# Experts of a mixture run in order of their load, with fewer rows for the less loaded ones

## The chip, the cores and the metric

The kernel runs on one core of one Trainium2 chip. The metric is the device time of one execution in microseconds, lower is better. A core has five engines that run side by side, each with a queue of its own that it works through in order: TensorE (PE in the profile) multiplies matrices, VectorE (DVE) and ScalarE (ACT) work element by element, GpSimd (POOL) does the same more slowly and issues gathers and scatters, SyncE (SP) issues transfers. Sixteen DMA engines move the data that those queues ask for. An instruction that must wait holds up everything behind it on its engine.

## The reference

The input has four batches of 512 tokens with 512 features. Three parts follow one another: a cross-attention of the normalised input, an attention block of 16 causal heads, and a mixture of experts. Only the last part is touched here. With T = 2048 tokens, 16 experts (E), 6 choices for each token (K) and a hidden width of 352 (I) it is:

```python
logits = t @ gate_w.T
probs = jax.nn.softmax(logits, axis=-1)
topv, topi = jax.lax.top_k(probs, K)
topv = topv / jnp.sum(topv, axis=-1, keepdims=True)
...
hh = jax.nn.silu(g) * u          # g = t @ eg_w[e].T, u = t @ eu_w[e].T
routed = jnp.einsum('eti,edi,te->td', hh, ed_w, cw)
shared = jax.nn.silu(t @ sg_w.T) * (t @ su_w.T) @ sd_w.T
out = x + (routed + shared).reshape(b, s, d)
```

Each token goes to its six best experts and, besides, through one shared expert of hidden width 704. On average an expert gets 2048 x 6 / 16 = 768 tokens.

## The kernel before

Every matmul is done in float16 with the operands split into a high and a low part, three products for one (`mm3`, L76 to L85: high x high, high x low, low x high). So each weight and each intermediate result is split by ScalarE, which writes the high part, and VectorE, which writes the low one (`split`, L69 to L71; `split1`, L73 to L75).

**Routing.** For each batch `route1` normalises the tokens, writes them split into `h2p` and transposes them into `h2T`. `route2` computes the logits on TensorE, the softmax (its Exp on ScalarE is L508) and the six best experts of each token. `route3` counts: a matmul with a triangular matrix gives each token its place among the tokens of an expert. `slot` is the row of the token in `xs_d`, a DRAM buffer with 2048 rows for each expert, `tid` the expert, `cw` the factor; each has one column for each of the six choices, in rising order of the expert's number. `macc` is the running count of tokens for each expert. GpSimd then scatters the rows to `xs_d` with one indirect DMA for 128 tokens and one choice (`scatter`, L452).

**Capacity.** An expert's rows are worked through up to a fixed number, `CAP` = 832. What is over goes through a conditional block at the end (`extra`, 60 blocks of 128 rows under a branch on `tot`), whose row and weight numbers are worked out on the chip from the counts (L848 to L892). It isn't entered unless an expert has more than 832 tokens.

**The expert loop** (L1073 and following). Experts run in the order of their number. For each, `static_weights` loads three pieces of weights with SP (L844) into `est` and splits them into `wt`, `wb` and `dt` on ScalarE and VectorE; `rows_in` has SP transpose the expert's rows from `xs_d` into `xT`, in two halves of 384 and 448 rows. `gate_up_rows` does, for each half, the gate and up projections (68 matmuls, with the rows as columns: 384 or 448 wide) and the product silu(g) x u; `down_rows` the down projection, nine 512-wide matmuls for each 128 rows and six for the 64 rows left over (L981), after which VectorE adds two parts (L984, L985). SP stores each block to `y_d`. The weights and rows of the next expert are fetched while one is worked on.

**Gathers.** Since a token's choices stand in rising order of the expert, its k-th choice is known to be stored once expert 10 + k is through. So from expert 11 on GpSimd gathers, for each of 16 groups of 128 tokens, one choice for each expert that is worked on (L1043), and VectorE adds it, times its factor, to the result (L1052). The sixth choice comes after the last expert.

**The shared expert** fills gaps: `shared(1, half)` and `shared(2, half)` lie between the routing of the last batch and expert 0, batch 3's at the end. In each half ScalarE does six Silus (L688), VectorE six products (L692 to L695) and both six splits (L73 to L75). Gate results take three PSUM banks in turn (tag `a`), up results two (tag `w`), so TensorE can run ahead of VectorE by that much only.

**What sets the order.** A scheduler places the instructions on each engine's queue by its own estimate of times; `after(x, y)` makes x stand behind y, and `pin` keeps an instruction in the order of the program. Buffers of a tag are taken in turn, and whoever writes one waits for the last reader of it.

Of the kernel before, what the change touches and what calls it, by code (L numbers as in the profile page):

```python
# [17 lines left out]
P = 128  # L18
# [13 lines left out]
SR = SI - 5 * P  # L32
LB = T // P
CAP = 832
FB = CAP // P
HB = CAP - FB * P
CUTS = (0, FB // 2 * P, CAP)
CW = CAP - CUTS[1]
ON = 60
ROWS = E * T + 1  # L40

# [11 lines left out]
def xattn_moe_block_kernel(ctx: ExitStack, tc: tile.TileContext, x, xT, ctxT, wqkx, bqk, ln1, ln2,  # L53
# [17 lines left out]
                nc.vector.scalar_tensor_tensor(lo, src, scale, hi, ALU.mult, ALU.subtract))  # L71

    def split1(hi, lo, src, eng=nc.vector):  # L73
        nc.scalar.activation(hi, src, AF.Copy)
        eng.tensor_tensor(lo, src, hi, ALU.subtract)  # L75

    def mm3(o, terms, start=True, stop=True, hold=None):
        n = len(terms)
# [54 lines left out]
    wo_d = [dram.tile([P, 2 * HG * D], F16, name=f"wo_d{g}") for g in range(G)]  # L133
    xs_d = dram.tile([ROWS, 2 * D], F16, name="xs_d")
    r_d = [dram.tile([P, NT, D], F32, name=f"r_d{b}") for b in range(B)]
    y_d = dram.tile([E * CAP + 1, D], F32, name="y_d")
    yo_d = dram.tile([ROWS, D], F32, name="yo_d")

    cw = const.tile([P, B * NT, K], F32, name="cw")
# [350 lines left out]
    def route2(b):  # L490
# [14 lines left out]
        nc.vector.tensor_reduce(mx, lgv, AX.X, ALU.max)  # L505
        pr = rp.tile([P, NT, E], F32, name="gpr", bufs=1)
        nc.vector.tensor_tensor(pr, lgv, mx.unsqueeze(2).to_broadcast([P, NT, E]), ALU.subtract)
        nc.scalar.activation(pr, pr, AF.Exp, scale=PSC)  # L508
        sm = rp.tile([P, NT], F32, name="gsm", bufs=1)
        nc.vector.tensor_reduce(sm, pr, AX.X, ALU.add)  # L510
        rc = rp.tile([P, NT], F32, name="grc", bufs=1)
# [160 lines left out]
    def gate_up(b, half, hid, tmp):  # L672
        shw = shx["w"]
        cl = slice(half * SH, (half + 1) * SH)
        hs = hid().rearrange("p (i a s) -> p i a s", i=6, a=2)
        for ic in range(6):
            R = P if ic < 5 else SR

            def proj(ps, a):
                o0 = ic * 8 * P + a * C * P  # L680
                mm3(ps, [(shw[:, 0, o0 + c * P:o0 + (c + 1) * P], shw[:, 1, o0 + c * P:o0 + (c + 1) * P],
                          h2T[b][:, c, cl], h2T[b][:, C + c, cl]) for c in range(C)])

            t = tmp()
            sg, hf = t[:, :SH], t[:, SH:]
            pg = bank("a", f"sg{b}_{half}_{ic}")[:, :SH]
            proj(pg, 0)
            nc.scalar.activation(sg[:R], pg[:R], AF.Silu, scale=PSC)  # L688
            if ic < 5:
                pu = bank("w", f"su{b}_{half}_{ic}")[:, :SH]  # L690
                proj(pu, 1)
                nc.vector.scalar_tensor_tensor(hf[:R], pu, GS * PSC, sg[:R], ALU.mult, ALU.mult)  # L692
            else:
                nc.vector.tensor_scalar(hf[:R], pg[R:2 * R], GS * PSC, None, ALU.mult)
                nc.vector.tensor_tensor(hf[:R], hf[:R], sg[:R], ALU.mult)  # L695
            split1(hs[:R, ic, 0], hs[:R, ic, 1], hf[:R])
            if ic == 5:
                nc.scalar.activation(hs[R:2 * R, ic, 0], hf[:R], AF.Copy)
        return hs
# [102 lines left out]
    route2(B - 1)  # L802
    route3(B - 1)
    scatter(B * NT * K)
    for half in range(2):
        shared(1, half)

    rctx.close()
    xin = ctx.enter_context(tc.tile_pool(name="xin", bufs=3, reuse_waits="tile"))
# [4 lines left out]
    GA = G2 - HB  # L814
    NA = C * GA

    def part(dsts, src, n, first=False):
        st_ = mw.tile([P, IP * 4], F32, tag="est", name="est", bufs=3)
        src(st_[:, :n])
        o = 0  # L820
        for hi, lo in dsts:
            w = math.prod(hi.shape[1:])
            v = st_[:, o:o + w]
            if len(hi.shape) == 3:
                v = v.rearrange("p (a b) -> p a b", a=hi.shape[1])
            for ins in split(hi, lo, v, WS):
                if first:
                    pin(ins)
            o += w

    def weights(load, first=False):
        wt = mw.tile([P, 2, NA], F16, name="wt")
        wb = mw.tile([P, C, 2, HB], F16, name="wb")
        dt = mw.tile([P, 2, 3 * D], F16, name="dt")
        for j in range(2):
            cl, ca = slice(j * 2, j * 2 + 2), slice(j * 2 * GA, (j + 1) * 2 * GA)
            part([(wt[:, 0, ca], wt[:, 1, ca]), (wb[:, cl, 0], wb[:, cl, 1])],
                 lambda o, j=j: load(o, (ew0, ew1)[j]), 2 * G2, first)
        part([(dt[:, 0], dt[:, 1])], lambda o: load(o, ed), 3 * D, first)
        return wt, wb, dt  # L840

    def static_weights(e):
        def load(dst, src):
            nc.sync.dma_start(dst, src[e * P:(e + 1) * P, :])  # L844
        return weights(load, e == 0)

    cps = bank("s", "cnt")
    nc.tensor.matmul(cps[:, :E], onesm, macc, start=True, stop=True)  # L848
    cnt = ms1.tile([P, E], F32, name="cnt")
    nc.vector.tensor_copy(cnt, cps[:, :E])  # L850
    NL = LB - FB
    thr = ms1.tile([P, NL], F32, name="thr")
    nc.vector.tensor_scalar(thr, ioe[:, FB:], float(P), float(CAP), ALU.mult, ALU.max)
    gt = ms1.tile([P, E, NL], F32, name="gt")
    nc.vector.tensor_tensor(gt, cnt.unsqueeze(2).to_broadcast([P, E, NL]),
                            thr.unsqueeze(1).to_broadcast([P, E, NL]), ALU.is_gt)
    mt = ms1.tile([P, E], F32, name="mt")
    nc.vector.tensor_reduce(mt, gt, AX.X, ALU.add)
    cs = mt
# [34 lines left out]
    xts = {}  # L894

    def rows_in(e, h):
        lo, hi = CUTS[h], CUTS[h + 1]
        t = xts[e, h] = xin.tile([P, 2 * C, hi - lo], F16, tag="xT", name="xT")
        flip(t, xs_d[1 + e * T + lo:1 + e * T + hi, :])

    nxt = static_weights(0)
    rows_in(0, 0)
    rows_in(0, 1)
    for half in range(2):
        shared(2, half)

    sf, tf = (v.rearrange("p t k -> p (t k)") for v in (slot, tid))
    rk, lt = (ms1.tile([P, B * NT * K], F32, name=nm) for nm in ("rkk", "rlt"))
    yru = ms1.tile([P, B * NT, K], U32, name="yru")
    yrc = ms1.tile([P, B * NT, K], U32, name="yrc")  # L910
    nc.vector.scalar_tensor_tensor(rk, tf, -float(T), sf, ALU.mult, ALU.add)
    nc.vector.tensor_scalar(lt, rk, float(CAP + 1), None, ALU.is_lt)
    nc.vector.scalar_tensor_tensor(rk, tf, float(CAP), rk, ALU.mult, ALU.add)
    nc.vector.tensor_tensor(rk, rk, lt, ALU.mult)
    nc.vector.tensor_copy(yrc.rearrange("p t k -> p (t k)"), rk)
    nc.vector.tensor_tensor(lt, sf, lt, ALU.mult)
    nc.vector.tensor_tensor(lt, sf, lt, ALU.subtract)
    nc.vector.tensor_copy(yru.rearrange("p t k -> p (t k)"), lt)

    RI = (P, P, I - 2 * P)  # L920
    pend = []
# [49 lines left out]
    def down_rows(dt, hT, lo, n, ll, put):  # L971
        ps = bank("s", f"y{lo}")
        yt = mp.tile([P, D], F32, name="yt")
        if n == P:
            mm3(ps, [(hT[:R, ic, lo:lo + P], hT[:R, ic, ll:ll + P],
                      dt[:R, 0, ic * D:(ic + 1) * D], dt[:R, 1, ic * D:(ic + 1) * D]) for ic, R in enumerate(RI)])
            nc.scalar.activation(yt, ps, AF.Copy, scale=1.0 / (GS * WS))
        else:
            for ic, R in enumerate(RI):
                for a in range(2):  # L980
                    nc.tensor.matmul(ps, hT[:R, ic, lo:lo + 2 * n], dt[:R, a, ic * D:(ic + 1) * D],  # L981
                                     start=ic == a == 0, stop=ic == 2 and a == 1)
            y2 = mp.tile([P, D], F32, tag="sb", name="y2")
            nc.scalar.activation(y2[:n], ps[n:], AF.Copy, scale=1.0 / (GS * WS))  # L984
            nc.vector.scalar_tensor_tensor(yt[:n], ps[:n], 1.0 / (GS * WS), y2[:n], ALU.mult, ALU.add)  # L985
        put(yt[:n])

# [5 lines left out]
    def expert(wd, e):  # L993
# [3 lines left out]
            return lambda yt: nc.sync.dma_start(y_d[r:r + yt.shape[0], :], yt)  # L997

        for h in range(2):
            w = CUTS[h + 1] - CUTS[h]  # L1000
            half = w % P
            hT = gate_up_rows(wt, wb, xts.pop((e, h)), w, half, tick)
            flush(tick)
            for lo in range(0, w, P):
                pend.append((dt, hT, lo, min(P, w - lo), w + half + lo, put(1 + e * CAP + CUTS[h] + lo)))
            yield

    def extra(o):
# [29 lines left out]
        ring.update(n=0, w=w, new=new, keep=keep)  # L1038

    def gather():  # L1040
        k, idx, src, tt = todo.pop(0)
        yg = place()
        nc.gpsimd.indirect_dma_start(out=yg, out_offset=None, in_=src,  # L1043
                                     in_offset=bass.IndirectOffsetOnAxis(ap=idx[:, tt, k:k + 1], axis=0))
        gathered.append((k, tt, yg))
        add(ring["keep"])

    def add(keep):
        while len(gathered) > keep:
            k, tt, yg = gathered.pop(0)  # L1050
            acc = residual(tt // NT)[:, tt % NT]
            pin(nc.vector.scalar_tensor_tensor(acc, yg, cw[:, tt, k:k + 1], acc, ALU.mult, ALU.add))  # L1052
            if k == K - 1 and tt not in late:
                store(tt, acc)

# [3 lines left out]
        if keep is not None:  # L1059
            add(keep)  # L1060

    def want(k, idx, src, tts=range(B * NT)):
        todo.extend((k, idx, src, tt) for tt in tts)

    def tick():
        left = ring["steps"]
# [6 lines left out]
    for e in range(E):  # L1073
        wd = nxt
        for h, _ in enumerate(expert(wd, e)):
            if h == 0 and e > E - K:
                gather_all()
                want(e - (E - K) - 1, yrc, y_d[:1 + e * CAP, :])
                ring["steps"] = 13
            if e + 1 < E:  # L1080
                rows_in(e + 1, h)
                if h == 0:
                    nxt = static_weights(e + 1)
    gather_all(0)
    lookahead(lambda: xin.tile([P, 3, D], F32, tag="xT", name="yg"), 3, 7)
    hs = shared_up(B - 1, 0)
    flush()
    want(K - 1, yrc, y_d)
    gather_all()
    shared_down(B - 1, 0, hs)  # L1090
    hs = shared_up(B - 1, 1)
# [4 lines left out]
    if stop is None or stop == "all":  # L1096
        rv = nc.values_load(tot[0:1, 0:1], min_val=0, max_val=E * NL)
        with tc.If(rv > 0):
            for o in range(ON):
                extra(o)  # L1100
            for k in range(K):
                want(k, yru, yo_d)
            gather_all(0)


# [61 lines left out]
```

## Time and profile before

| | us |
|---|---|
| median of the timed runs | 1899.01 (1898.14 to 1901.34) |
| profiled execution | 1826.83 |
| its span, first to last instruction | 1825.1 |
| mean granted TensorE clock in it | 0.985 |
| TensorE busy | 1747.9 |
| VectorE busy | 1122.9 |
| ScalarE busy | 843.8 |
| GpSimd busy | 441.0 |

All views of the trace are of the one profiled execution. Places in it are in us from the span's start. A line such as L844 is a line of the kernel's file; where a helper like `split` or `mm3` issues an instruction, the line is the helper's, so the three products of `mm3` stand under L80, L83 and L84. A row of groups names engine, operation, output and inputs, shape, count, busy time and mean duration; a row of waits names who waited for whom, the sum, how often and the longest. TensorE's instructions overlap: their durations are longer than the distance from one start to the next. "Clock" is the share of full speed that TensorE was granted.

### The profile page before, as it was taken

Reading aid. Unit: us, or ns where it says so; the run is one execution under the profiler, and the core shown is the slowest. Engines: PE = TensorE matmul, PEld = TensorE weight load, DVE = VectorE, ACT = ScalarE, POOL = GpSimd, SP = SyncE. Lnnn points to the kernel's source line nnn. Section 1 sums busy time; section 2 is a strip of 40 time slices with the busy share of each in tenths; the row PEclk is TensorE's granted clock in tenths of the full one; section 3 lists DMA queues with packets and bytes.
Section 4 is the critical chain, followed back from the end, with each engine's and each line's share of the span. In section 5 each row is a group of like instructions: output and inputs, shape, how many; then the busy total and the mean of one; then the engine's idle time right before and its main releaser. Section 6 shows DMA issues by size and latency. Waiting matters only on the chain. (4 is left out here: it accounts for less than half of the span.)

```text
span 1825.1 us, 28676 instructions
## 1 busy us (share of the span) xinstructions
PE 1747.9 (96%) x10483; PEld 990.7 (54%) x10483; DVE 1122.9 (62%) x2784; ACT 843.8 (46%) x1769; POOL 441.0 (24%) x522
## 2 busy tenths in 40 slices
PE   8899899999999999899999999899999999999997
PEld 3555455555555555556556757555555555554554
DVE  6887777777776667666667545344334434456655
ACT  4655645465534545445455522345444444444322
POOL 5423011130345353000003635000000000044553
PEclk9999999999999999999999999999999999999999
DMA  7978668574678578534446646455555565599756
GB/s 237 242 157 226 148 145 188 149 193 95 142 170 237 146 160 237 102 66 94 100 97 143 182 120 208 130 145 149 166 156 150 140 176 142 147 246 234 204 171 209
DMA packets 398294, 298.78 MB, mean 164 GB/s; under 512 B 339840, under 2 KB 340096, under 8 KB 397376
## 3 DMA queue, kind: packets, MB, share of 16 engines
q1 hardware_dynamic: 365024, 182.81, 43.0%
q0 software_dynamic: 33120, 114.06, 19.8%
q8 instruction: 84, 1.38, 0.3%
q14 instruction: 66, 0.54, 0.1%
HBM read 124.81 MB, written 90.18 MB: 118 GB/s over the span
## 5 line engine op out<-in xcount | busy, mean ns | idle before, releaser
L1043 POOL DMA_INDIRECT yg<-y_d,yrc x96 | 107.6, 1121 | 577.9 <-DVE hf L946 470.4
L627 ACT ACTIVATE pe<-pe,bnm 128x128 f32<-128x128 f32 (+3 forms) x256 | 142.4, 557 | 160.7 <-DVE bnm L625 160.0
L80 PE MATMUL qk<-hT,wqk 128*128 128x512 f16 (+1 forms) x520 | 196.2, 377 | 3.8 <-DMA hT<-hh 3.8
L84 PE MATMUL qk<-hT,wqk 128*128 128x512 f16 (+1 forms) x520 | 196.3, 377 | 0.0
L83 PE MATMUL qk<-hT,wqk 128*128 128x512 f16 (+1 forms) x520 | 196.2, 377 | 0.0
L71 DVE SCALAR_TENSOR_TENSOR pn<-pe,brc,pn 128x128 f16<-128x128 f32 (+3 forms) x256 | 147.4, 585 | 21.8 <-ACT pn L70 18.8
L625 DVE CUSTOM_DVE_ANT_0 pe<-sc,causal 128x128 f32<-128x128 f32 (+3 forms) x256 | 117.1, 485 | 58.5 <-PE sc L622 58.0
L70 ACT ACTIVATE pn<-pe,brc 128x128 f16<-128x128 f32 (+3 forms) x256 | 133.5, 553 | 30.6 <-ACT pe L627 18.5
L80 PE MATMUL v<-wv,hT 128*128 128x256 f16 x512 | 139.7, 273 | 0.9 <-DMA hT<-hh 0.9
L83 PE MATMUL v<-wv,hT 128*128 128x256 f16 x512 | 139.7, 273 | 0.0
L84 PE MATMUL v<-wv,hT 128*128 128x256 f16 x512 | 139.6, 273 | 0.0
L80 PE MATMUL g<-xT,wt 128*128 128x384 f16 (+1 forms) x384 | 130.3, 339 | 0.0
L83 PE MATMUL g<-xT,wt 128*128 128x384 f16 (+1 forms) x384 | 130.3, 339 | 0.0
L84 PE MATMUL g<-xT,wt 128*128 128x384 f16 (+1 forms) x384 | 130.2, 339 | 0.0
L932 ACT ACTIVATE hT_e<-hf 128x384 f16<-128x384 f32 (+2 forms) x96 | 52.6, 548 | 141.1 <-DVE hf L946 140.2
L70 ACT ACTIVATE qkt<-qk 128x512 f16<-128x512 f32 x128 | 74.8, 586 | 80.2 <-PE qk L84 79.3
L80 PE MATMUL y<-dt,hT_e 128*128 128x512 f16 (+1 forms) x288 | 109.9, 382 | 0.0
L84 PE MATMUL y<-dt,hT_e 128*128 128x512 f16 (+1 forms) x288 | 109.2, 379 | 0.0
L83 PE MATMUL y<-dt,hT_e 128*128 128x512 f16 (+1 forms) x288 | 109.1, 379 | 0.0
L659 DVE SCALAR_TENSOR_TENSOR x<-wo,x 128x512 f32<-128x512 f32 x128 | 87.4, 686 | 29.5 <-PE wo L84 28.9
L80 PE MATMUL av<-pt,vt 128*128 128x512 f16 (+3 forms) x256 | 78.5, 307 | 26.8 <-DMA pt<-pn 13.9
L452 POOL DMA_INDIRECT xs_d<-h2p,slotu x96 | 96.6, 1006 | 28.8 <-issue 26.7
(293 smaller groups left out, 4204.1 us busy)
## 6 DMA issues: line engine op xcount, KB each, us to landing
y_d<-yt SPq DMA_DIRECT2D x96, 256.0 KB, 2.8
est<-in_ew_dram SPq DMA_DIRECT2D x32, 704.0 KB, 6.5
est<-in_ed_dram SPq DMA_DIRECT2D x16, 768.0 KB, 4.2
wqk<-wqk_d POOLq DMA_DIRECT2D x20, 512.0 KB, 4.5
wqk_st<-in_wqk_dram SPq DMA_DIRECT2D x16, 512.0 KB, 4.2
wqk_d<-wqk POOLq DMA_DIRECT2D x15, 512.0 KB, 5.5
xs_d<-causal POOLq DMA_DIRECT2D x16, 384.0 KB, 6.4
wv<-wv_d POOLq DMA_DIRECT2D x10, 512.0 KB, 4.1
```

The lines of the kernel that those rows point to most:

```text
L70: return (nc.scalar.activation(hi, src, AF.Copy, scale=scale), nc.vector.scalar_tensor_tensor(lo, src, scale, hi, ALU.mult, ALU.subtract))
L71: nc.vector.scalar_tensor_tensor(lo, src, scale, hi, ALU.mult, ALU.subtract))
L80: ins = nc.tensor.matmul(o, lh, rh, start=start and j == 0, stop=False)
L83: nc.tensor.matmul(o, lh, rl, start=False, stop=False)
L84: ins = nc.tensor.matmul(o, ll, rh, start=False, stop=stop and j == n - 1)
L452: ins = nc.gpsimd.indirect_dma_start(out=xs_d, out_offset=bass.IndirectOffsetOnAxis(ap=slotu[:, tt, k:k + 1], axis=0), in_=h2ps[tt], in_of ...
L625: nc.vector.tensor_tensor_reduce(pe, ps[:, :w], causal[:, S - w:], -1.0, 3e38, ALU.add, ALU.min, nm)
L627: nc.scalar.activation(pe, pe, AF.Exp, bias=nm, scale=-1.0, accum_out=sm)
L659: nc.vector.scalar_tensor_tensor(x2[:, t, :], ps, 1.0 / (VS * WS), x2[:, t, :], ALU.mult, ALU.add)
L932: nc.scalar.activation(hT[:R, ic, :w], hf, AF.Copy)
L1043: nc.gpsimd.indirect_dma_start(out=yg, out_offset=None, in_=src, in_offset=bass.IndirectOffsetOnAxis(ap=idx[:, tt, k:k + 1], axis=0))
```

## The change

The experts are ranked on the chip by their count of tokens, the fullest first. The loop runs over ranks, and the rank decides how many rows are worked through: 832 for ranks 0 to 2, 800 for 3 to 9, 768 for 10 to 15. Which expert has a rank is read into registers of SP (`seat`), and the addresses of the weight loads and of the row transposes are worked out from them. Since results lie in `y_d` in order of rank, each token's six rows and factors are sorted by rank before the gathers. The Exp of the last batch's routing softmax and the splits of the second expert's weights get another place in the order. The diff, cut to its core ("...": left out):

```diff
-FB = CAP // P
-HB = CAP - FB * P
-CUTS = (0, FB // 2 * P, CAP)
-CW = CAP - CUTS[1]
+STEPS, DC = (3, 10), 32
+CAPS = [CAP - DC * sum(r >= s for s in STEPS) for r in range(E)]
+OFFS = [1 + sum(CAPS[:r]) for r in range(E + 1)]
+FB = min(CAPS) // P
+CUT = FB // 2 * P
+CW = CAP - CUT
+HB = 64
...
     scatter(B * NT * K)
+
+    cps = bank("s", "cnt")
+    nc.tensor.matmul(cps[:, :E], onesm, macc, start=True, stop=True)
+    cnt = const.tile([P, E], F32, name="cnt")
+    nc.vector.tensor_copy(cnt, cps[:, :E])
+    key = rp.tile([P, E], F32, tag="gmx", name="key", bufs=1)
+    nc.vector.scalar_tensor_tensor(key, cnt, float(E), ioe, ALU.mult, ALU.subtract)
+    sq = rp.tile([P, E, E], F32, tag="w4", name="sq", bufs=1)
+    nc.vector.tensor_tensor(sq, key.unsqueeze(1).to_broadcast([P, E, E]),
+                            key.unsqueeze(2).to_broadcast([P, E, E]), ALU.is_gt)
+    rank = const.tile([P, E], F32, name="rank")
+    nc.vector.tensor_reduce(rank, sq, AX.X, ALU.add)
...
+    nc.vector.tensor_reduce(whof, sq, AX.X, ALU.add)
+    who = const.tile([1, E], I32, name="who")
+    nc.vector.tensor_copy(who, whof[0:1, :])
...
     for half in range(2):
         shared(1, half)
+    after(zz["exp"], zz["silu", 1, 0, 1])
...
-            for ins in split(hi, lo, v, WS):
-                if first:
+            for j, ins in enumerate(split(hi, lo, v, WS)):
+                if order == 0:
                     pin(ins)
+                elif order == 1:
+                    after(ins, zz["hs", 2, 1][j])
...
-    def static_weights(e):
+    here = {}
+
+    def seat(r):
+        here[r] = nc.values_load(who[0:1, r:r + 1], engines=[mybir.EngineType.SP], min_val=0, max_val=E - 1)
+
+    def ranked_weights(r):
         def load(dst, src):
-            nc.sync.dma_start(dst, src[e * P:(e + 1) * P, :])
-        return weights(load, e == 0)
+            nc.sync.dma_start(dst, src[bass.ds(here[r] * P, P), :])
+        return weights(load, r)
...
     def rows_in(e, h):
-        lo, hi = CUTS[h], CUTS[h + 1]
-        t = xts[e, h] = xin.tile([P, 2 * C, hi - lo], F16, tag="xT", name="xT")
-        flip(t, xs_d[1 + e * T + lo:1 + e * T + hi, :])
+        lo, n = h * CUT, CAPS[e] - CUT if h else CUT
+        t = xts[e, h] = xin.tile([P, 2 * C, n], F16, tag="xT", name="xT")
+        flip(t, xs_d[bass.ds(here[e] * T + (1 + lo), n), :])
...
+    n = NT * K
+    for b in range(B):
+        oh = mp.tile([P, CW], F32, tag="sg", name="roh")[:, :n * E].rearrange("p (n e) -> p n e", e=E)
+        ts = slice(b * n, (b + 1) * n)
+        nc.vector.tensor_tensor(oh, tf[:, ts].unsqueeze(2).to_broadcast([P, n, E]),
+                                ioe.unsqueeze(1).to_broadcast([P, n, E]), ALU.is_equal)
+        nc.vector.tensor_tensor(oh, oh, rank.unsqueeze(1).to_broadcast([P, n, E]), ALU.mult)
+        nc.vector.tensor_reduce(rt[:, ts], oh, AX.X, ALU.add)
+    nc.vector.scalar_tensor_tensor(yr, rt, float(CAP), rk, ALU.mult, ALU.add)
+    for s_ in STEPS:
+        nc.vector.tensor_scalar(lt, rt, -float(s_), 0.0, ALU.add, ALU.max)
+        nc.vector.scalar_tensor_tensor(yr, lt, -float(DC), yr, ALU.mult, ALU.add)
...
+    for t in range(B * NT):
+        nc.vector.max(m8[:, t, :], ng[:, t, :])
+    nc.vector.tensor_scalar(m8, m8, -1.0, None, ALU.mult)
+    nc.vector.tensor_copy(yrc, m8[:, :, :K])
...
+        nc.vector.tensor_tensor(eq, yv[:, ts].unsqueeze(2).to_broadcast([P, NT, K, K]),
+                                m8[:, ts, :K].unsqueeze(3).to_broadcast([P, NT, K, K]), ALU.is_equal)
+        nc.vector.tensor_tensor(eq, eq, cw[:, ts].unsqueeze(2).to_broadcast([P, NT, K, K]), ALU.mult)
+        nc.vector.tensor_reduce(cws[:, ts], eq, AX.X, ALU.add)
...
-            w = CUTS[h + 1] - CUTS[h]
+            w = CAPS[e] - CUT if h else CUT
...
-                want(e - (E - K) - 1, yrc, y_d[:1 + e * CAP, :])
+                want(e - (E - K) - 1, yrc, cws, y_d[:OFFS[e], :])
...
             if e + 1 < E:
+                if h == 0:
+                    seat(e + 1)
                 rows_in(e + 1, h)
                 if h == 0:
-                    nxt = static_weights(e + 1)
+                    nxt = ranked_weights(e + 1)
```

In the order that the scheduler makes of it, the sixteen register loads of SP stand together: the first ahead of rank 0's weight loads, the other fifteen right behind these, ahead of the first row transposes. The two first `roh` products stand in VectorE's queue among the last steps of `route1`, ahead of the last batch's last transpose; the rest of the ranking and sorting stands between the reduction of `tid` (L569 before) and the splits of rank 0's weights, among the products and splits of shared(1) and shared(2). The matmuls of the loop, the scatters and the gathers keep their order.

## The prediction

> **What bounds the kernel now.** I read the page first, then the chain that ended last, then TensorE's waits by stage, then stretches of the span, then single instructions. The page says TensorE:
>
> ```profile
> PE 1747.9 (96%) x10483; PEld 990.7 (54%) x10483; DVE 1122.9 (62%) x2784; ACT 843.8 (46%) x1769; POOL 441.0 (24%) x522
> ```
>
> An average over stages decides nothing, so the expert stage next. In the chain of work, in order of time, the six matmuls of an expert's last 64 rows (L981) come back at an even beat; the stretch between two of them is one expert. The columns of the second view are busy time and count of PE, PEld, DVE, ACT, POOL, then granted clock, DMA share, GB/s.
>
> ```profile
> 1331.89 1.30 PE y L981 x6
> 1368.78 1.30 PE y L981 x6
> ```
>
> ```profile
> 1331.89:1368.78 36.89, 36.89 (x197) 19.14 (x196) 15.36 (x25) 16.78 (x29) 0.00 (x0) 1.00 0.56 153
> 1627.03:1663.93 36.90, 36.90 (x198) 19.15 (x196) 22.57 (x36) 15.79 (x28) 17.79 (x15) 1.00 0.98 248
> ```
>
> One expert is 36.89 us, TensorE never pauses, the clock is full, every other engine is busy at most 61%. Here a column less is time less. In the second row, with gathers running, the DMA engines are 0.98 busy: little is spare. What a column costs is the distance of starts in the timeline (us, duration, line, operation):
>
> ```profile
> 1339.83 0.35 PE L83 MATMUL u<-xT,wt 128*128 128x448 f16 x1
> 1340.02 0.35 PE L84 MATMUL u<-xT,wt 128*128 128x448 f16 x1
> ...
> 1351.13 0.33 PE L83 MATMUL g<-xT,wt 128*128 128x384 f16 x1
> 1351.30 0.33 PE L84 MATMUL g<-xT,wt 128*128 128x384 f16 x1
> ```
>
> The 0.35 and 0.33 overlap; from start to start over a dozen it is 0.1887 us at 448 columns and 0.1625 at 384, so 32 columns are 0.0131 us.
>
> Ahead of the experts, between routing the last batch and expert 0 (its first matmul starts at 1173.70), TensorE does wait. Its waits between 1045 and 1180, and the stretches where they fall:
>
> ```profile
> PE sy L80 <- ACT hs L74: 6.9, 1, 6.9
> PE sg L80 <- ACT sgt L688: 3.8, 1, 3.8
> ```
>
> ```profile
> 1075.00:1080.00 5.00, 1.18 (x20) 0.89 (x21) 2.42 (x19) 3.48 (x5) 1.39 (x2) 0.84 0.20 54
> 1080.00:1085.00 5.00, 5.00 (x25) 3.41 (x24) 3.52 (x13) 1.49 (x4) 2.68 (x9) 0.50 0.16 56
> ...
> 1140.00:1145.00 5.00, 0.51 (x5) 0.20 (x3) 0.00 (x0) 0.00 (x0) 0.00 (x0) 0.83 1.12 272
> 1145.00:1150.00 5.00, 2.57 (x9) 1.22 (x10) 2.37 (x4) 2.49 (x5) 0.00 (x0) 0.50 0.80 289
> ```
>
> The first wait: ScalarE stands at the routing softmax's Exp (with a table load of 1.28 us before and after it), and shared(1)'s Silu stands behind it. The second: ScalarE stands at expert 1's weight split (L70) until 1145.60, because that load sits in SP's queue behind the row transposes, which wait for the scatter; shared(2)'s split (L74) stands behind. After both the clock is 0.50, so each costs more than its idle time: 4.25 us idle (5.00 - 4.57 in the stretch from 1070, 5.00 - 1.18 above) and 2.5 at half clock; 6.9 + 0.5 idle and 1.3 at half clock.
>
> **What the Trainium skill says.** "TensorE: Matmul & The Clock Gate", Back-to-back issue gap: N/2.4 + 2.5 ns warm, so 162.5 ns at 384 and 189.2 at 448; the trace agrees (162.5, 188.7). Same page, The HAM clock gate: after an idle window of about 3.4 us the array runs at half rate until it has been busy as long; the 0.50 above agrees. "DMA: Bandwidth & Descriptors", Latency and other measured facts: a tensor_load has a floor of some 600 ns; the one that SP makes here takes less:
>
> ```profile
> L1097 SPq TENSOR_LOAD <-tot x1: 476/476/476, 1141.3 to 1141.3; - x1
> ```
>
> No page prices a DMA whose address comes from a register, and the trace of before has none.
>
> **The change, part by part.** *Rows.* Ranks 0 to 2 keep 832, ranks 3 to 9 have 800, ranks 10 to 15 have 768. An expert's second half has 68 gate and up matmuls (4 x 12 + 12 + 8). At 416 columns: 68 x 0.0131 = 0.89 us less; the down projection of the odd rows keeps its six 512-wide matmuls. At 384: 68 x 0.0262 = 1.78, and the six (1.30) go: 3.08. Sum 7 x 0.89 + 6 x 3.08 = **24.7 us**, all on TensorE in a stage where it is never idle. It is only good if no expert overflows: the reference's counts, sorted, are 822, 820, 817; 796 down to 751; 747 down to 705. The closest is 4 rows under its limit, so the conditional stays untaken.
>
> *Exp behind the Silu.* Stall one goes: ScalarE does three Silus first, TensorE goes on. Against it: two of the new `roh` products (0.71 us each, the row of `oh`) stand in VectorE between the last h2 steps, and delay the last transpose and so the logits by some 0.8. Gain 6.7 - 0.8 = 5.9; shared(2) then starts at 1114, not 1120. The scatters, which follow from the rank products, start some 4 us earlier too: there the half clock and a VectorE copy behind a Silu product held them.
>
> *Expert 1's splits behind shared(2).* Stall two, 8.7 us, goes. The splits (VectorE 5.2, ScalarE 4.4) lie then under the last down projection of shared(2) (34 x 0.2155 = 7.3); were that cover gone, they would cost up to 5.
>
> *Ranking and sorting.* VectorE gets some 20 us: 8 products of 128x384 at 0.71, 4 reductions at 0.55, 5 steps 256 wide at about 0.43 (between the rows for 160 and 384), 16 Max at 0.1, 8 products and 4 reductions of 144 at 0.32, some 25 smaller at 0.15 to 0.26. `sq` takes the buffer of `w4`, so the ranking starts only after `tid` is reduced (1112.4 before; 1108.4 with the scatters 4 us earlier). By VectorE's order, `who` is written 9 us on, 1117.5; the evacuation of shared(2)'s first up bank comes at 1124.9, 16.5 after `tid`. TensorE starts shared(2) at 1114, has two up banks, does five groups of 12 x 0.109 = 6.5 and stands at 1120.4: 4.5 us. After that VectorE leads: its list as far as the last split of half 0, with rank 0's own weight split (5.2) in it, ends at about 1147. What TensorE has left is 108 x 0.109 + 38 x 0.2155 = 20.0, so 1167, and a microsecond at half clock: expert 0 at 1168 instead of 1173.7. The stage nets **5.7 us** of the 14.6 freed.
>
> *Register loads and addresses.* `who`, then rank 0's three weight loads (issued by 1120.5, landing in 4.9 median: under VectorE's list), then on SP 15 more loads of 0.48 + 0.19 + 0.03, with gaps 0.8 each: 12 us. Behind them on SP stand the three row transposes (11.9 us on SP before) and rank 1's weights: 1145, landing by 1155, where 1167 is early enough. In the loop there is one register step ahead of each of five DMAs an expert, under 0.2 each by the 0.19 above, on a queue with some 20 idle us an expert. From below a register address costs nothing; from above, if the two transposes took twice their 3.5 us on SP, the queue would still have 13 us to spare. I take 0.
>
> *Sorted choices.* As many gathers, as many rows, in the same places; only addresses and factors differ. But the last six experts, where the gathers run, become 3.08 shorter with the same bytes. There TensorE waits already:
>
> ```profile
> PE u L955 <- DVE hf L946: 3.6, 2, 2.8
> ```
>
> VectorE stood at a sum whose gather was late. 2.5 us at half clock follow. I take **1.7 us** more of this; bounds: 6 less (the stalls vanish) to 15 more (the beat doesn't shrink).
>
> *Tail.* After the last expert's last block there is no second evacuation (VectorE 0.69): **0.7**. From there on 16 gathers on POOL set the end, as before.
>
> Sum: 24.7 + 5.7 - 1.7 + 0.7 = 29.4 us against the profiled execution's 1826.83 (span 1825.1, 1.7 around it): 1797.4. The median of the timed runs is 1899.01, 72 above it, and the trace doesn't show why. If that is fixed, 1869.6; if all scales by 1.04, 1868.4. I take 1869.6; under 0.2% (3.8 us) a measurement of this kernel couldn't tell from no change.
>
> **Rivals.** *All is kept.* VectorE's list turns out shorter or TensorE's banks suffice, and the gathers stay out of the way: 14.6 + 24.7 + 0.7 = 40, so 1859. For it: the small VectorE operations overlap (starts 0.07 apart where independent). Against: two up banks are two. *The gather stage keeps its beat.* The DMA engines at 0.98 carry the same bytes per expert; the five experts with gathers save nothing: 15.4 less, 1885. For it: that share, and sums waiting 31 us for gathers. Against: from 1705 on the share is mostly 0.45 to 0.8 at the same beat, and 5 us stretches show up to 400 GB/s against 248. *Slower: expert 0 waits for SP.* The 15 register loads stand ahead of the first row transposes. At 0.8 us each they are hidden. Expert 0 would have to start 23.7 us later than before (24.7 - 1.7 + 0.7), at 1197: then the transposes (17 with landing) can't begin before 1180, and from 1120.5 that is 4.0 us a load, five times my 0.8. At 4.8 the end would be 12 later than before: 1911. *The change doesn't do what it says:* an expert over its limit would run 60 extra blocks, hundreds of us; the counts speak against it.
>
> **How the numbers follow.** Forecast 0.63, all kept 0.15, beat kept 0.14, SP slower 0.05, a mix of late VectorE and late gathers that leaves within 0.2% 0.03. The first three are faster: 0.92; same 0.03; slower 0.05. The likeliest alone, with the stage netting 3 to 9 and the gathers costing 0 to 6: 1865 to 1877. The range goes to both neighbours: 1857 to 1884.
>
> **What would show it.** The beat by rank: 36.9, 36.0, 33.8 us; other beats in the first ten experts make the column term wrong. TensorE waiting in shared(2) for `sgt` at about 1120, no waits at 1076 and 1141, and expert 0 at 1168: if it starts after 1174, the ranking costs more than I say. SP's first row transpose about 1133. In the last six experts, more wait of `u` for `hf`. I would be wrong if register addresses make the transposes slow enough to reach TensorE in each expert.

## The result

The kernel after takes 1881.28 us (median of 16 runs, 1872.80 to 1899.91), the kernel before 1899.55 beside it (16 runs, 1891.47 to 1923.03). The ratio is 0.991, with an interval from 0.9883 to 0.9937: 12 to 22 us less, 18 by the medians. Two later sets gave 0.9916 (0.9880 to 0.9951) and 0.990 (0.9859 to 0.9940). Forecast were 1869.6 and 29.4 less. So the sign is right, the time lies in the range (1857 to 1884), but 4 us above the likeliest case's own range, and 11 of the 29 are missing.

The profiled execution of before (1826.83) and one set of experiments (before 1827.83 there) lacked certain unnamed waits of TensorE, which every other set showed (before 1894 to 1902). The first is called the quiet condition below, the second the usual one. No edit sets it: before alone shows both, and one chip showed the usual condition in one set and the quiet one in the next. Stages are compared only within one condition.

The page of after, in the usual condition (busy time, share of the span and instructions of each engine):

```profile
PE 1755.6 (94%) x10447; PEld 990.5 (53%) x10447; DVE 1122.0 (60%) x2822; ACT 837.6 (45%) x1763; POOL 443.1 (24%) x522
```

Stretches of after, one beat each: at 832 and at 800 rows from the six products of one expert's last rows to the next expert's; then three at 768 rows, which have no such six and are cut to the length of the beat, the last two with gathers beside them (columns: busy time and count of PE, PEld, DVE, ACT, POOL; granted clock, DMA share, GB/s):

```profile
1281.02:1317.91 36.89, 36.89 (x197) 19.14 (x196) 15.36 (x25) 16.83 (x29) 0.00 (x0) 1.00 0.55 152
1390.73:1426.94 36.21, 36.21 (x197) 19.05 (x198) 15.03 (x25) 16.98 (x29) 0.00 (x0) 1.00 0.54 153
1607.92:1641.70 33.78, 33.78 (x189) 18.40 (x190) 14.52 (x22) 15.76 (x28) 0.00 (x0) 1.00 0.53 153
1675.50:1709.30 33.80, 33.80 (x191) 18.55 (x190) 21.00 (x32) 13.18 (x23) 17.58 (x15) 1.00 1.00 267
1709.30:1743.10 33.80, 28.11 (x152) 15.25 (x151) 20.55 (x31) 12.90 (x22) 13.12 (x12) 0.90 0.96 203
```

TensorE is never idle in the first four; in the fifth it loses 5.7 us, and the clock falls to 0.90.

The span cut where three instructions start: the last logits product, the first gate product of expert 0, and the last gate product of expert 15 that is high x high (the first of `mm3`'s three). "Rest" is what lies behind it.

| kernel | to the logits' end | to expert 0 | expert stage | rest | span |
|---|---|---|---|---|---|
| before, quiet (the forecast's) | 1075.4 | 98.2 | 580.9 | 70.6 | 1825.1 |
| before, usual (e1) | 1114.9 | 109.3 | 578.1 | 82.2 | 1884.5 |
| after, usual | 1128.7 | 104.7 | 561.3 | 82.1 | 1876.8 |
| after, usual (e6) | 1132.0 | 101.7 | 562.6 | 74.1 | 1870.4 |
| after, usual (e13) | 1133.6 | 103.1 | 558.1 | 77.6 | 1872.4 |

### The profile page after: what moved, and what is told of

It is laid out like the page before. It is cut to its first block, busy times and chain, and to the rows that moved or that the text cites. A ratio compares the mean times of both kernels' runs of the same rounds, so it can differ in the third digit from the quotient of the medians.

```text
span 1876.8 us, 28785 instructions
## 1 busy us (share of the span) xinstructions
PE 1755.6 (94%) x10447; PEld 990.5 (53%) x10447; DVE 1122.0 (60%) x2822; ACT 837.6 (45%) x1763; POOL 443.1 (24%) x522
## 5 line engine op out<-in xcount | busy, mean ns | idle before, releaser
L87 PE MATMUL v<-wv,hT 128*128 128x256 f16 x512 | 141.5, 276 | 6.9 <-issue 6.8
L83 PE MATMUL v<-wv,hT 128*128 128x256 f16 x512 | 141.6, 276 | 6.7 <-issue 5.6
L86 PE MATMUL v<-wv,hT 128*128 128x256 f16 x512 | 141.4, 276 | 4.9 <-issue 4.6
L83 PE MATMUL g<-xT,wt 128*128 128x384 f16 (+2 forms) x384 | 127.3, 332 | 0.0
L86 PE MATMUL g<-xT,wt 128*128 128x384 f16 (+2 forms) x384 | 127.3, 331 | 0.0
L87 PE MATMUL g<-xT,wt 128*128 128x384 f16 (+2 forms) x384 | 127.2, 331 | 0.0
L73 ACT ACTIVATE qkt<-qk 128x512 f16<-128x512 f32 x128 | 75.0, 587 | 86.7 <-PE qk L87 82.1
L999 ACT ACTIVATE hT_e<-hf 128x384 f16<-128x384 f32 (+3 forms) x96 | 51.0, 532 | 136.6 <-DVE hf L1013 123.2
L74 DVE SCALAR_TENSOR_TENSOR qkt<-qk,qkt 128x512 f16<-128x512 f32 x128 | 87.6, 686 | 22.5 <-ACT qkt L73 18.5
```

The lines of the kernel that those rows point to most:

```text
L73: return (nc.scalar.activation(hi, src, AF.Copy, scale=scale), nc.vector.scalar_tensor_tensor(lo, src, scale, hi, ALU.mult, ALU.subtract))
L83: ins = nc.tensor.matmul(o, lh, rh, start=start and j == 0, stop=False)
L86: nc.tensor.matmul(o, lh, rl, start=False, stop=False)
L87: ins = nc.tensor.matmul(o, ll, rh, start=False, stop=stop and j == n - 1)
L999: nc.scalar.activation(hT[:R, ic, :w], hf, AF.Copy)
```

## The experiments

**Before once more (e1)**, nothing edited.

> The kernel before, unchanged, profiled once more: its first profiled execution (1826.83) is 72 us below its timed median. If that execution was the odd one, this one takes 1885 to 1905, and the extra 60 to 70 us lie ahead of the shared expert on batch 1 (there the profile after is 51 us later than the first profile of before, with 104 us of TensorE waits marked issue), and some in the stage before expert 0. Theory A (the forecast's stalls are real in a typical execution): the waits sy for hs (6.9) and sg for sgt (3.8) at about the same distance from expert 0 are there again. Theory B (in a typical execution TensorE is held in that stage by waits marked issue while the scatters run): those two waits are smaller than in the first profile, and sg and su wait for issue 10 us or more between the end of the logits and expert 0.

The profiled execution took 1886.33. TensorE's waits between the logits' end and expert 0 (1114.9 to 1224.2; line, what it waited for, us in total, times, longest):

```profile
PE sg L80 <- issue: 5.2, 6, 1.3
PE sg L80 <- ACT sgt L688: 3.8, 1, 3.8
PE sg L84 <- issue: 2.6, 4, 0.8
PE sg L83 <- issue: 2.0, 3, 1.0
PE su L84 <- issue: 1.9, 3, 1.0
```

"issue" is a wait for nothing that the profile names. The stall behind Exp (3.8) is there as in the forecast's profile. The larger one, `sy` for `hs` with 6.9, is not: TensorE comes to it later than ScalarE does. Both theories were half right. Where TensorE is held is the stretch in which GpSimd issues its 24 scatters; the same stretch in the forecast's profile, then in e1, then in after:

```profile
1095.00:1126.63 31.63, 31.63 (x239) 22.85 (x237) 14.89 (x51) 10.81 (x22) 24.74 (x25) 1.00 0.60 225
```

```profile
1133.60:1165.13 31.53, 20.75 (x119) 11.75 (x117) 4.31 (x9) 2.40 (x6) 24.64 (x25) 0.71 0.49 192
```

```profile
1144.90:1176.37 31.47, 20.64 (x119) 11.59 (x119) 4.19 (x9) 2.40 (x6) 24.52 (x25) 0.73 0.51 192
```

The scatters take the same 31.5 us each time. TensorE does 239 products in it in the quiet condition and 119 in the usual one, at a clock of 0.7. 120 products fewer, at 0.109 each, are 13 us, and this stage differs by 11 between the two profiles of before. The quiet profile had none of it.

The 119 are an average of two parts. For the first 10.5 us of its stretch e1 isn't held at all; from there on it gets 39 products in 20 us:

```profile
1133.60:1144.10 10.50, 10.50 (x82) 7.68 (x80) 2.61 (x5) 1.19 (x3) 8.06 (x9) 1.00 0.46 177
1144.10:1164.10 20.00, 10.06 (x39) 4.07 (x37) 1.28 (x3) 0.82 (x3) 15.62 (x16) 0.57 0.51 197
```

The other batches' scatters meet such waits too. Of e1's 62 us of unnamed waits of TensorE, 55 lie where GpSimd issues a batch's scatters or the last gathers, or within 6 us behind; in the quiet profile it is 5 of 15. That the two fall together in time is shown; that the scatters cause the waits is not, since no run moved or thinned them.

**Rows alone (e3)**: before, with each expert's width written in by its known count. The rows of `y_d` that are no longer computed are zeroed by 13 DMAs on GpSimd in the attention stage.

```
CAPE = [768 if c <= 768 else 800 if c <= 800 else CAP for c in CNT]
-            w = CUTS[h + 1] - CUTS[h]
+            w = (CUTS[1], CAPE[e])[h] - CUTS[h]
+        n = CAP - CAPE[e]
...
+            after(nc.gpsimd.dma_start(yd, causal[:, :n * D // P]), zz["pad"])
```

> Before with the shorter rows alone: every expert has the 832, 800 or 768 that its known count allows, written into the program; no ranking, no registers, no sorting, no order edit; y_d keeps its places, and the rows that are no longer computed are zeroed by 13 small DMAs early. Leaves out the choice of widths on the chip. Theory A (the column term is right, only its size a little off): beats 36.9, 36.2, 33.8 and 22 to 25 us less than before, ratio 0.987 to 0.9885. Rival (the gather stage keeps its beat): the five experts with gathers stay at 36.9 on the mean, 10 to 15 us less.

Measured 1862.44 (6 runs), ratio 0.9786 (0.9735 to 0.9838). My expectation was wrongly worked out: by count, three experts need 832, four 800 and nine 768 (the counts 768, 765 and 751 fit in 768, though ranks 7 to 9 get 800), so the beats promise 4 x 0.69 + 9 x 3.09 = 30.6 and not 23. The interval, 31 to 50 less, begins there. The traced execution had 554.7 in the expert stage. All at 832 take 575.3 there (e4); less 30.6, of which 1.3 fall behind the stage, that is 546.0, so 8.7 are lost again.

**Rows alone, nothing early (e7)**: the same widths and no zeroing DMAs; the rows of `y_d` not computed are filled by a second store of the last block on SP.

```
+                nc.sync.dma_start(y_d[r + yt.shape[0]:r + yt.shape[0] + n, :], yt[:n])
```

> The shorter rows alone once more, but the rows of y_d that are no longer computed are filled by a second store of the last block's rows on SP in the expert stage, so nothing ahead of the experts differs from before (leaves out the choice of widths on the chip). Theory A (rows are worth 23.4, and the 37 measured with the early zeroing had some 13 us from elsewhere): 20 to 27 us less than before. Rival (rows alone really are worth 37, and the rest of the change costs 19): 32 to 42 us less.

Measured 1866.93 (6 runs) against 1894.28, ratio 0.9856 (0.9809 to 0.9903), 18 to 36 less, around the 30.6 (theory A's 20 to 27 came from the 23.4, which is wrong for these widths). The traced expert stage is 546.3 against 546.0 worked out: the whole column gain, kept in this profile. What e3 showed beyond that was not settled (its early DMAs, or few runs).

**Everything but the rows (e4)**: `STEPS, DC = (E, E), 32`, so all ranks have 832.

> After with all ranks at 832 rows: ranking, register addresses, sorted choices and both order edits stay, the shorter rows go. Theory A (the order edits free more than the ranking costs): 3 to 9 us less than before. Theory B (what the order edits free is not to be had in a typical execution, or the ranking eats it): within 3 us of before, or up to 10 us more.

1897.40 (22 runs) against 1899.21, ratio 0.9989 (0.9964 to 1.0014). Ranking, registers, sorting and order edits together move the time by -7 to +3. The trace has 104.2 to expert 0, as after, and an expert stage of 575.3 without any stall, gathers and sorted addresses included. So a register address costs the loop nothing, and sorting by itself doesn't disturb the gathers. The total doesn't decide between the theories. The stage ahead of expert 0 is 5 us shorter than e1's, but that isn't the order edits' doing (e8).

**The order edits alone (e5)**: before plus `after(zz["exp"], zz["silu", 1, 0, 1])` and expert 1's splits after the last `hs` of shared(2).

> Before with the two order edits alone (Exp behind the third Silu; expert 1's splits behind the last product of the shared expert on batch 2). Theory A: 12 to 15 us less than before, expert 0 that much nearer to the end of the logits. Theory B: 0 to 6 us less, because the stalls are covered by waits marked issue in a typical execution.

1902.96 (22 runs), ratio 1.0029 (1.0005 to 1.0054): not faster, if anything slower. TensorE's waits between the logits' end and expert 0:

```profile
PE su L83 <- issue: 6.2, 6, 1.5
PE sg L80 <- ACT sgt L688: 3.2, 1, 3.2
PE sg L83 <- issue: 2.7, 3, 1.3
```

Here Exp stands behind exactly two Silus, and TensorE stands at the third bank instead of the first: the wait has moved, not gone. The splits had no stall to remove. Theory A falls; theory B's 0 to 6 less is missed too, by a little.

**After without the order edits (e8)**: both lines taken out of after.

> After with both order edits undone (Exp where the scheduler puts it, expert 1's splits where before had them). Theory A as forecast (the edits free 14.6, of which the ranking eats 8.9): 5 us or more slower than after. Theory B (the stretch ahead of expert 0 is set by the scatters, during which TensorE gets a third of its rate, so the edits are worth nothing): within 3 us of after, total 1878 to 1885.

1880.02 (22 runs) against 1894.28, ratio 0.992 (0.9896 to 0.9944), where after has 0.9916 in the same set (e6); 104.9 to expert 0. In the usual condition the two edits are worth nothing, as theory B said. ScalarE's order shows a reason for one of them: in e8, as in after, Exp stands behind three Silus. With the new VectorE work around it, the scheduler puts it there unasked. What removes the stall is the schedule that the whole change brings. In the quiet condition neither edit was taken out alone.

**After once more (e6)**, nothing edited.

> The kernel after, unchanged, profiled once more. Theory A (the chip's own waits in the stretches where scatters and gathers are issued back to back make up the variation): total 1873 to 1900; logits' end between 1120 and 1135; from there to expert 0's first matmul 103 to 107; beats 36.9, 36.2, 33.8. The gather stage is the open point: its first profile lost 8 to 9 us in one wait for a late gather. If that belongs to the change (the same bytes in shorter experts), it is 5 to 10 again; if it was that execution's accident, 0 to 3, as in the profiles with all experts at 832 (0) and with the short rows alone (1 to 3).

1876.60 (8 runs) against 1894.28, ratio 0.9916 (0.9880 to 0.9951). The expert stage lost 562.6 - 553.2 = 9.4 (553.2 is e4's 575.3 less the 22.1 of the columns that fall in it), again with one wait of 5.7:

```profile
PE u L1022 <- DVE hf L1013: 5.7, 1, 5.7
```

The third profile of after (e13) lost 4.9, e8 13.1. Of the usual kernels with 832 rows, e4 lost 0, e5 and e9 0.5 and e1 2.8. So most of it belongs to the shorter rows. VectorE stands at sums whose gathers are late, and `hf`, which TensorE waits for from 1719.9 to 1725.6 in after, stands behind them and a weight split of 1.8:

```profile
1718.34 0.75 DVE L1119 SCALAR_TENSOR_TENSOR acc<-yg,cws,acc 128x512 f32<-128x512 f32 x1 [4.11 <-DMA yg<-y_d,yrc]
...
1722.47 0.75 DVE L1119 SCALAR_TENSOR_TENSOR acc<-yg,cws,acc 128x512 f32<-128x512 f32 x1 [2.44 <-DMA yg<-y_d,yrc]
1723.29 1.76 DVE L74 SCALAR_TENSOR_TENSOR dt<-est,dt 128x1536 f16<-128x1536 f32 x1
1724.97 0.55 DVE L1013 SCALAR_TENSOR_TENSOR hf<-u,sg 128x384 f32<-128x384 f32 x1
```

The second choice's gathers meet DMA engines at 1.00 in after; at the same place of e4 the two beats are:

```profile
1684.61:1721.50 36.89, 36.89 (x197) 19.15 (x196) 25.97 (x41) 16.77 (x28) 20.87 (x16) 1.00 0.92 251
1721.50:1758.40 36.90, 36.90 (x198) 19.15 (x196) 24.52 (x40) 16.43 (x28) 19.88 (x18) 1.00 0.84 234
```

**Slots one by one (e10, e11)**: in after and in before, gathered rows reuse their six slots singly.

```
-    lookahead(lambda: st2.tile([P, 3, D], F32, tag="hs", name="yg"), 3, 4)
+    slots = [st2.tile([P, 3, D], F32, tag="hs", name="yg") for _ in range(2)]
+    lookahead(turn, 3, 5)      # turn: the two tiles in turn
```

> After with one edit in the gather stage: the six slots that gathered rows land in are reused slot by slot (two tiles of three kept for good, five gathers ahead of the sums), not three at a time. Theory C (the stall of u for hf is a late gather: a gather is issued late because it waits until all three slots of a tile have been summed, and VectorE's sum, and with it hf and TensorE, waits for it): the wait of 5.7 goes, the stage from expert 0 to the last up product takes 553 to 556 instead of 561 to 563, and the total is 5 to 9 us less than after, ratio to before 0.986 to 0.988. Rival (the DMA engines at 1.0 are the bound there): the wait stays at 5 or more and the total is within 2 us of after.

> Before with the same edit of the slots. Theory C: before lost only 0 to 3 us in that stage, so 0 to 3 less than before. Rival (slot reuse matters everywhere, and its gain has nothing to do with the shorter rows): 5 us or more less than before.

This set met the quiet condition: before 1827.83 (27 runs), e10 1806.51 (6 runs, ratio 0.9885, 0.9833 to 0.9938), e11 1833.87 (22 runs, 1.0035, 1.0010 to 1.0060). The edit helps neither: e11 is slower than before, and in e10 the wait is still there, with 563.6 in the expert stage, 10.4 over 553.2:

```profile
PE u L1022 <- DVE hf L1013: 6.5, 2, 3.9
```

Theory C falls; the slots are not the cause. That the full DMA engines are it remains the reading that fits: cut into beats from just ahead of the first gather on, every profile that lost 4.9 or more has a beat at 0.98 to 1.08, while e4, e7 and e11, which lost nothing or 0.3, stay at 0.96 or less. But e5 and e9 reach 0.98 and 0.97 and lost 0.5, and no run took load off the engines. Why the same short rows lose 8.7 in e3 and 0.3 in e7, one profile each, isn't shown. So the cause stays open in part.

More was learned from the stage ahead of expert 0 in these two. TensorE's waits there in e11 (before, but for the slots) and in e10 (after, but for the slots), quiet condition both:

```profile
PE sy L80 <- ACT hs L74: 6.1, 1, 6.1
PE sg L80 <- ACT sgt L688: 3.8, 1, 3.8
```

```profile
PE sy L715 <- ACT hs L701: 0.8, 1, 0.8
PE xixp L921 <- DVE xixd L919: 0.7, 1, 0.7
PE wixp L921 <- DVE wixd L919: 0.6, 1, 0.6
```

Both stalls of the forecast are real in that condition, both are gone after the change, and 2.1 us of small waits stand in their place. The stage takes 97.0 in e11 and 84.8 in e10: 12.2 less.

**A longer ranking (e12)**: 30 multiplications by one, in a chain, ahead of the sum that gives `who`.

```
+    for _ in range(30):
+        nc.vector.tensor_scalar(sq, sq, 1.0, None, ALU.mult)
```

> After with 30 idle multiplications by one, each behind the other, put into the ranking ahead of the sum that gives who: some 9 to 10 us more of VectorE work there, and who, the register loads and the row transposes later by as much. Theory of the forecast (TensorE stands on VectorE's list in the shared expert on batch 2): expert 0's first matmul comes 8 to 11 us later after the end of the logits than in after (103), at 111 or more. Theory B (TensorE is late by itself, held while the scatters are issued, so the list is hidden): 102 to 106.

In the same set, one execution took 1801.52. Each of the 30 takes 0.28, so 8.4 us more of VectorE, and `who` is written at 1147.9, 31.5 after `tid` (6.9 in e10), with the row transposes behind it (1150.8). Expert 0 starts 83.9 after the logits' end, against 84.8 in e10. TensorE's waits in between:

```profile
PE sy L715 <- ACT hs L701: 0.8, 1, 0.8
PE su L83 <- DVE sgt L695: 0.2, 1, 0.2
```

So the list is hidden even with 8.4 us more in it, and a `who` 25 us later does no harm. The scheduler strews the 30 among shared(2)'s own operations, where my 8 to 11 us had them in one piece: its first up bank is evacuated 13.1 after `tid`, against 12.4 in e10. In the quiet condition TensorE isn't late by itself, so the reason that theory B gave isn't the one. VectorE's work in e10 from `tid` on (start, duration, line, operation) shows it:

```profile
1124.69 0.55 DVE L572 TENSOR_REDUCE tid<-w 128x24 f32<-128x384 f32 x1 [4.46 <-POOL w L571]
1125.16 0.41 DVE L695 SCALAR_TENSOR_TENSOR sgt<-su,sgt 128x256 f32<-128x256 f32 x1
1125.49 0.41 DVE L816 TENSOR_TENSOR sq<-key 128x256 f32<-128x256 f32 x1
...
1131.56 0.16 DVE L826 CAST who<-whof 1x16 int32<-1x16 f32 x1
...
1137.10 0.42 DVE L695 SCALAR_TENSOR_TENSOR sgt<-su,sgt 128x256 f32<-128x256 f32 x1
```

The ranking is woven between the shared expert's own operations. The last line is the evacuation that TensorE needs, 12.4 after `tid`. VectorE doesn't pause between the two: the durations of the 43 operations from `tid` on add up to 15.6, but each starts before the one ahead of it has ended, so they take 12.4. And products of 128x384 take 0.55, not the 0.71 that I had priced.

**Twice the instructions (e9)**: before, with the second half of shared(1) in matmuls of 128 columns.

```
+                cuts = (0, SH // 2, SH) if (b, half) == (1, 1) else (0, SH)
+                for u, v in zip(cuts, cuts[1:]):  mm3(ps[:, u:v], ...)
```

> Before with each matmul of the shared expert on batch 1, second half (132 of 256 columns) made as two of 128, so twice the instructions for the same columns; everything else as before. It leaves out nothing. In that half TensorE steps at 0.70 us a matmul while the scatters are issued. If an instruction costs that (TensorE is short of instructions), the half takes 15 to 25 us longer and expert 0 starts 15 to 25 us further from the end of the logits than the 109 of before. If the columns cost it (the array or its memory is slowed), the half takes 0 to 5 us longer.

One execution, usual condition: 1892.72, expert 0 115.0 after the logits' end, 5.7 more than e1. That is between the two expectations, just above the second. The scatters' stretch tells more, whole and then cut where the holding starts:

```profile
1143.10:1174.36 31.26, 15.33 (x126) 9.02 (x124) 2.59 (x5) 1.18 (x3) 24.38 (x25) 0.66 0.50 194
```

```profile
1143.10:1149.40 6.30, 6.30 (x71) 4.25 (x70) 1.74 (x3) 0.38 (x1) 4.97 (x5) 1.00 0.43 168
1149.40:1169.40 20.00, 7.65 (x54) 4.33 (x51) 0.85 (x2) 0.80 (x2) 15.58 (x16) 0.60 0.51 197
```

While held, TensorE gets 54 products of 128 columns in 20 us, where e1 got 39 of 256. If the columns had set the pace, it would have been twice as many; so the hold goes mostly by the instruction. It also sets in by their number rather than by time: after 71 products here and 82 in e1, though these took 6.3 and 10.5 us. My 15 to 25 forgot that the stretch has an end. What isn't done in it (20.75 - 15.33 = 5.4 us of busy time) is done after it.

**After a last time (e13)**, nothing edited.

> The kernel after, unchanged, beside before once more. In the last set before took 1827.8, as in the profiled execution that the forecast was worked from, and TensorE waited for nothing unnamed while the scatters were issued. If before takes 1820 to 1835 again, the forecast's own sum applies: 1797.4, that is 29.4 less, ratio 0.984; by what the other runs showed (columns 23.4, gathers 5 more than forecast, the ranking hidden or not) 1797 to 1805, ratio 0.983 to 0.988, with expert 0 92 to 95 after the end of the logits where before had 98. If before takes 1890 to 1900, the result is as it was: 17 to 18 less, ratio 0.990 to 0.992.

The condition was the usual one: 1884.56 (6 runs) against 1902.24, ratio 0.990 (0.9859 to 0.9940). After itself was therefore never run in the quiet condition; e12 (one execution, with needless work added) and e10 stand for it there with 26 and 21 less than before.

## Why the prediction was right and wrong

*Rows.* Right, a little too high: the beats are 36.89, 36.20 and 33.80, so 7 x 0.69 + 6 x 3.09 = 23.4 against 24.7. At 800 rows an expert saves 0.69 and not 0.89; 0.12 of that is that the six products of the last 32 rows take longer than those of the last 64:

```profile
1354.75 1.30 PE y L1048 x6
1390.73 1.42 PE y L1048 x6
```

(chain of after, the end of an 832 beat and of an 800 beat). I had left these six at one cost.

*Stage before expert 0.* In the sum right, but by luck, for its terms are wrong. Forecast were 5.7 less. Usual condition: 109.2 (e1, e3 and e7, which share these instructions: 109.3, 109.3, 108.9) to 103.2 (three profiles of after), 6.0 less. But of the terms 5.9 and 8.7 freed and 8.9 lost only the first exists there. The other two, which nearly cancelled each other, are both absent: no `sy` wait to remove, and nothing paid for the ranking. Quiet condition, in which I had priced it: 97.0 to 84.8, so 12.2 less. Both stalls went, and the failed step is the evacuation of shared(2)'s first up bank "16.5 after `tid`", from which I had TensorE stand 4.5 us and VectorE lead to the end. It comes at 12.4 (e10), and the ranking cost some 2, not 8.9 (e10, e12). The order of VectorE's list was read rightly; the price was wrong. I had added up durations (15.6, and 6 x 0.16 for products priced too dear, make about the 16.5), where the distance of starts counts, by which I had priced TensorE's products. And 0.71 was the longest of four such products in the forecast's own profile; the others took 0.56:

```profile
L526 DVE TENSOR_TENSOR oh<-ix,ioe x4: 557/558/712, 527.2 to 1081.3; 128x384 f32<-128x384 f32 x4
```

The rival "all is kept" nearly described this stage there, and its reason, that small VectorE operations overlap, is what e10 shows.

*Register loads.* Right that they are hidden, a little too dear: 0.26 us each and 0.72 apart, not 0.48 and 0.8 (SP's loads of `who` in after, min/median/max in ns):

```profile
L878 SPq TENSOR_LOAD <-who x16: 262/264/466, 1186.4 to 1197.2; - x16
```

The first row transpose starts at 1198.8, 34.6 before expert 0, where 17 were early enough in e12. The slower rival (4.0 us a load) was far away. Register addresses cost the loop nothing: e4's beats are 36.9 throughout.

*Gathers.* This is the term that was mis-sized: 1.7 more forecast, with 6 less to 15 more as its bounds. After lost 8.1, 9.4 and 4.9 in its three profiles (mean 7.5), the 832-row kernels of the same condition 1.0 on the mean (e1, e4, e5, e9): 6.5 more. The rival "the gather stage keeps its beat", worth 15, was half true; the place (`hf` behind a late sum) and the sign were right, and the reason, full DMA engines, fits but isn't shown. Of the 31 us that sums wait for gathers, counted for that rival, only 15 lie in the expert stage (1590 to 1760); the rest is behind it.

*Tail.* Forecast 0.7; the rest is 77.9 on the mean of three against 79.5 of the four with 832 rows, and 1.3 of these 1.6 belong to the columns. Smaller than the spread.

*Sum.* -23.4 - 6.0 + 6.5 - 0.3 = -23.2 by the traces, where the timed runs give -18 (12 to 22). *"If that is fixed"*, the step from 1826.83 to the median, held only roughly: of the 59.4 between the two profiles of before, 39.5 lie ahead of the logits' end, where the change does nothing, but 11.1 lie in the stage that it edits, and change what is to be gained there, and 11.6 in the rest.

The last 5 us are not settled. The profiles point ahead of the logits' end: five with after's code (after, e4, e6, e8, e13) end them at 1127 to 1139, five with before's code (e1, e3, e5, e7, e9) at 1115 to 1132. Some 7 of the 8 between the means are there already at the first logits of batch 0 (532.1 against 525.0), where before and after have given every engine the same instructions so far. In the quiet condition the two don't differ there (522.4 and 528.4 in e10 and e12, 521.8 and 530.5 in before and e11). No run tells why.

## What to carry over

A profile is one execution: when its own time lies 4% below the median, the stalls in it may not be those of the median, so profile again before pricing an edit that removes a wait. A stall of one profile can be missing in another because the engine has been held elsewhere by then (the 6.9 of `sy`, absent in e1), while columns taken from a matmul that never waits came back one for one (e7). Where a scheduler weaves a new list into old work, read the woven order before charging the list in one piece (e12), and price it by the distance of starts, not by durations (15.6 against 12.4 in e10).

## What the runs showed of the hardware

While GpSimd issues indirect DMAs back to back, TensorE may get through only 119 products in 31.5 us where 239 are done otherwise. The waits are unnamed and the clock falls to 0.7. TensorE first goes on unheld for some 80 products; then it gets 39 in 20 us, or 54 when most have half the columns (e1, e9). Whether this happens belongs to the moment: one chip showed both within two consecutive sets, and before differed by 66 us between them. It is seen in the dense 256-column products; in e1's experts, with 80 gathers beside them, TensorE had no unnamed wait.

The obvious suspect is the supply of instructions. The Trainium skill, "Runtime: NRT & Kernel Launch", Instruction fetch mechanics, says that a sequencer fetches its instructions in 16 KiB blocks, 256 instructions each, over a DMA queue of its own, and that this is mostly hidden. The trace has such a queue. Between the first and the last of the 24 scatters it carries one such packet in e1, which took 0.93 us, and two in the quiet profile, of 1.21 and 1.07. That speaks against a slow transfer; when a packet was asked for, the trace doesn't show. Slow weight loads aren't the cause either: those of the shared expert take 0.12 each in e1's held part and 0.10 in the quiet stretch. So the count of products speaks for the supply, and nothing here proves it.
